# Attention in four layers on one core: keys gathered ahead of values and turned two steps ahead, the weights' loads put into the hand-kept order, a copy of the tokens moved

## The chip, the cores and the metric

The kernel runs on one core of a Trainium2 chip. Its time is the device time of one execution in microseconds (us). The engines are TensorE (PE, with its weight loads PEld), VectorE (DVE), ScalarE (ACT), GpSimd (POOL) and SyncE (SP), which issues most of the DMAs. POOL issues the gathers.

## The reference

```python
x = x + _L0_ffn_ref(_L0_cond_ref(x, ...), ...)
x = x + _L1_ffn_ref(_L1_cond_ref(x, ...), ...)
x = x + _L2_ffn_ref(_L2_cond_ref(x, ...), ...)
x = x + _L3_ffn_ref(_L3_cond_ref(x, ...), ...)
```

The tokens x are 8 sequences of 128 tokens with 512 features, float32. Each layer is a conditioning part and a feed-forward part with low-rank experts. The change is about `_L2_cond_ref`, attention with a paged cache:

```python
def _L2_cond_ref(x, Wq, Wk, Wv, Wo, q_norm_w, k_norm_w, k_cache, v_cache, block_table, cache_seqlens):
    D, HQ, HK = (128, 32, 8)
    PAGES, PSIZE, NPP = (64, 32, 16)
    ...
    q = _rope(_rmsnorm(q, q_norm_w), pos); k = _rope(_rmsnorm(k, k_norm_w), pos)
    L = NPP * PSIZE
    kc = k_cache[block_table].reshape(bsz, L, HK, D)
    vc = v_cache[block_table].reshape(bsz, L, HK, D)
    k_all = jnp.concatenate([kc, k], axis=1)
    v_all = jnp.concatenate([vc, v], axis=1)
    ...
    scores = jnp.einsum('bqhd,bkhd->bhqk', q, k_all) * SCALE
    scores = jnp.where(valid[:, None, None, :], scores, -1e+30)
    probs = jax.nn.softmax(scores, axis=-1)
    o = jnp.einsum('bhqk,bkhd->bqhd', probs, v_all)
    return jnp.einsum('bse,de->bsd', o.reshape(bsz, seqlen, HQ * D), Wo)
```

Per sequence there are 512 cached keys and values and 128 new ones, 32 query heads and 8 key heads.

## The kernel before, in words

Layers 0 and 1 come first (to about 330 us of the span), then attention, then the feed-forward part of layer 2 and layer 3. Attention is written out in 32 steps: 8 key heads (`qd`), and for each the 4 pairs of sequences (`p`, two sequences j = 0, 1). Step n works on `steps[n]`; `S[n]` holds its tiles. One key head has 4 query heads.

A step of `run` (L1227), in the order of TensorE's work:
- `weigh(n, 0)` (L1091): five score tiles `st` of the first sequence, four of cached keys `kT` and one of the new keys `kn` (in the profile `kTn`), against the queries `qT`. ScalarE takes the exponentials to `pT`, VectorE adds them up (`added`, L1113, tiles `part`).
- `project(n+1)` (L980): queries, keys and values of the next step, as a seven-product scheme for 2x2 blocks (`seven`, L932, PSUM tiles `q_one`, `q_six`, `q_five`, three buffers of the tag `mm`). Each block sum is taken from PSUM by VectorE or ScalarE in a fixed place; the dictionary `at` names calls that come between the products ("six", "u1", "u2", "c22", "c11", "c12"). The row sums of step n (`summed`, `inverted`, `spread`: a reciprocal `rr`, four copies to `R`, three DMAs that spread `R` over the partitions, one to `sums`) stand in these places too, and so does `turn_cached(n+1)` at "c22".
- `rotate(n+1)` (L1021): rotary embedding, products of POOL (`vq`, `vk`) and of VectorE (`r`), put together by `rotated` and `normed` inside the next part.
- `leave(n-1)` (L1169): the product with Wo of the step before, again with seven products (`wo_one`, `wo_two`, `wo_six`). At its "c22" stands `turn(n+1)` (L1077): VectorE transposes 32x32 blocks to `qkt`, SP writes them in four DMAs to a DRAM array `turned_new` and reads them back as `qT` and `kTn`.
- `weigh(n, 1)` with the value products `av` of the first sequence between its score tiles, the second sequence's sums, and its value products.

The cached keys come by `gather(n, "k")` (L887): 8 indirect DMAs of POOL into `kn`, two buffers. `turn_cached(n)` (L1061) transposes them on VectorE to `kt` (one buffer, shared with `qkt`), writes `turned_cached` and loads `kT` (two buffers). `gather(n, "v")` brings the values into `vals`. Before, POOL's order in a step is: `vq`, `vk` of n+1, two additions to `y`, values of n+1, keys of n+2.

Weights: `weights(qd)` (L876) loads three parts of one tile `q7` (Wk 256 KB, Wq 1 MB, Wv 256 KB) for the next head; `factors` (L867) makes four differences of blocks on VectorE. `out_weights(qd)` (L882) loads 1 MB of Wo, with four differences of its own. Both tiles have one buffer. `combine` (L904) makes four such sums of the tokens or of the outputs.

What sets the order: a scheduler of the tile layer places instructions on each engine by its own estimate of when they can start, but those wrapped in `kept(...)` are to stay in program order among themselves:

```python
def kept(i):
    return tc.keep_in_program_order(i) if running or i.ins.engine == pool.engine else i
```

`running` is filled when the step loop starts. Before, the weights' loads are not wrapped, while the DMAs of `turn`, `turn_cached` and `spread` are. `kept_x` (L716) is a copy of x in DRAM, 2 MB, for a second path that is taken only when a row sum is out of range.

Of the kernel before, what the change touches and what calls it, by code (L numbers as in the profile page):

```python
# [17 lines left out]
P = 128  # L18
# [29 lines left out]
def forward(ctx: ExitStack, tc: tile.TileContext, a: dict, out: bass.AP):  # L48
# [615 lines left out]
    with psa:  # L664
# [48 lines left out]
        mix1(1, small_bank)  # L713
        outs1(1, range(DC), large_bank)
        kept = nc.dram_tensor("kept_x", (P, DC, NT), F32, kind="Internal").ap()
        sp.dma_start(kept, x)  # L716
        c1.close()
        cl = ExitStack()
        late = cl.enter_context(tc.tile_pool(name="late", bufs=1, side="right"))
# [6 lines left out]
            lambda shape, name: ww.tile(shape, F32, tag="q7", name=name),  # L726
            lambda shape, name: ww.tile(shape, F32, tag="qs", name=name), chunks, mm,
        )
        y2 = att.run(late, end, bank)
        c2.close()  # L730
        c3 = ExitStack()
        w3 = c3.enter_context(tc.tile_pool(name="w3", bufs=1, reuse_waits="tile"))
# [51 lines left out]
def attention(tc, a, x, ident, lens, kvrow, part, ww, wop, ypool, sums, rot, eps, psa, c2, chunks, mm):  # L784
# [75 lines left out]
    def blocks(dst_pool, tag, name, n):  # L860

        raw = dst_pool.tile([P, 4, 2 * n], F32, tag=tag + "7", name=name)
        sums_ = dst_pool.tile([P, 4, 2, n], F32, tag=tag + "s", name=name + "_s")
        b11, b12, b21, b22 = (raw[:, 2 * i : 2 * i + 2, j * n : (j + 1) * n] for i in range(2) for j in range(2))
        t1, t2, t3, t4 = (sums_[:, k] for k in range(4))

        def factors():  # L867
            for o, l, r in ((t1, b12, b11), (t2, b22, t1), (t3, b22, b12), (t4, b21, t2)):
                kept(dve.tensor_tensor(o, l, r, ALU.subtract))

        return SimpleNamespace(raw=raw, factors=factors, B=(b11, b21, b22, t1, t2, t3, t4))

# [2 lines left out]

    def weights(qd):  # L876
        W[qd] = w = blocks(ww, "q", f"q7_{qd}", KW)
        sp.dma_start(w.raw[:, :, 0:HD], chunks(a["WkT"])[:, :, qd * HD : (qd + 1) * HD])
        sp.dma_start(w.raw[:, :, HD : HD + 2 * HW], chunks(a["WqT"])[:, :, qd * REP * HD : (qd + 1) * REP * HD])
        sp.dma_start(w.raw[:, :, HD + 2 * HW :], chunks(a["WvT"])[:, :, qd * HD : (qd + 1) * HD])  # L880

    def out_weights(qd):  # L882
        h0 = qd * REP * HD
        WO[qd] = w = blocks(wop, "o", f"o7_{qd}", HW)
        sp.dma_start(w.raw, a["WoT"][h0 : h0 + REP * HD, :].rearrange("(h p) o -> p h o", p=P))

    def gather(n, what):  # L887
        qd, p = steps[n]
# [15 lines left out]
    def combine(t, a11, a12, a21, a22):  # L904

        s1, s2, s3, s4 = (t[:, k] for k in range(4))
        for o, l, r, op in (
            (s1, a21, a22, ALU.add), (s2, s1, a11, ALU.subtract),
            (s3, a11, a21, ALU.subtract), (s4, a12, s2, ALU.subtract),
        ):  # L910
            kept(dve.tensor_tensor(o, l, r, op))
        return a11, a12, a22, s1, s2, s3, s4

    kept_sums = {}

    def tokens(n):


        qd, p = steps[n]
        b = 2 * p  # L920
        if 0 < qd < NQ - 1 and p in kept_sums:
            S[n]["A"] = kept_sums[p]
            return
        parts = [x[:, 2 * h : 2 * h + 2, (b + j) * P : (b + j + 1) * P] for j in range(2) for h in range(2)]
        if 0 < qd < NQ - 1:
            if not kept_sums:
                late.append(late[0].tile([P, NP, 4, 2, P], F32, tag="yT", name="xs_all"))
            S[n]["A"] = kept_sums[p] = combine(late[1][:, p], *parts)
        else:
            S[n]["A"] = combine(wk.tile([P, 4, 2, P], F32, tag="xs", name=f"xs_{n}", bufs=1), *parts)  # L930

    def seven(A, B, name, u, two, out2, out4, c11, c12, c21, c22, at):  # L932

# [87 lines left out]
    def rotate(n):  # L1021

        both = wk.tile([P, 2 * REP + 2, HD], F32, tag="r", name=f"r_{n}", bufs=1)
        views = {"q": both[:, 0 : 2 * REP], "k": both[:, 2 * REP :]}

        def terms(m, t, nh):

            full, part_ = [P, 2, nh, HD], [P, 2, nh, 64]
            ws, wx = (w[:, pair(n), :] for w in tabs[m])
            r = views[m].rearrange("p (j h) d -> p j h d", j=2)  # L1030
            u = wk.tile(full, F32, tag="v" + m, name=f"v{m}_{n}", bufs=1)
            for lo, hi in ((0, 64), (64, 0)):
                kept(pool.tensor_tensor(  # L1033
                    u[:, :, :, lo : lo + 64], t[:, :, :, hi : hi + 64],
                    wx[:, :, lo : lo + 64].unsqueeze(2).to_broadcast(part_), ALU.mult,
                ))
            kept(dve.tensor_tensor(r, t, ws.unsqueeze(2).to_broadcast(full), ALU.mult))
            return r, u

        for m, nh in (("q", REP), ("k", 1)):  # L1040
            S[n]["r" + m] = terms(m, S[n][m], nh)
        S[n]["both"] = both
# [34 lines left out]
    def turn(n):  # L1077

        s = S[n]
        m = 2 * REP  # L1080
        t = wk.tile([P, 4, m + 2, 32], F32, tag="kt", name=f"qkt_{n}", bufs=1)
        kept(dve.transpose(t, s["both"].rearrange("p m (b d) -> p b m d", b=4)))  # L1082
        s["qT"] = wk.tile([P, 4, m, 32], F32, tag="qT", name=f"qT_{n}", bufs=1)
        s["kn"] = wk.tile([P, 2, 4, 32], F32, tag="kTn", name=f"kTn_{n}", bufs=1)
        written(turned_new[n], t)
        src = turned_new[n].rearrange("b i a m d -> (b i) a m d")
        kept(sp.dma_start(s["qT"], src[:, :, 0:m, :]))
        for j in range(2):
            kept(sp.dma_start(s["kn"][:, j], src[:, :, m + j, :]))
# [71 lines left out]

    def outputs(n):
        oT = S[n]["oT"]
        S[n]["oA"] = combine(
            late[0].tile([P, 4, 2, P], F32, tag="os", name=f"os_{n}"),
            *(oT[:, j, 2 * h : 2 * h + 2, :] for j in range(2) for h in range(2)),
        )

    def leave(n, at={}):  # L1169

# [34 lines left out]
    def begin():  # L1205
        weights(0)
        out_weights(0)
        gather(0, "k")
        gather(0, "v")
        gather(1, "k")  # L1210
        W[0].factors()

    def first(n):
        tokens(n)
        project(n)
        if n == 0:
            turn_cached(n)
        for j in range(2):
            squares(n, "q", j, range(REP))
            squares(n, "k", j, range(1))  # L1220
        rotate(n)
        roots(n)
        rotated(n)
        normed(n)
        turn(n)

    def run(pool_, end, bank):  # L1227
        late.append(pool_)
        y2 = ypool.tile([P, NB, D], F32, tag="y", name="y2")
        Y.append(y2)  # L1230
# [3 lines left out]
        running.append(True)  # L1234
        end.prepare(bank)
        tokens(2)
        WO[0].factors()
        for n, (qd, p) in enumerate(steps):

            after = n + 1 if 0 < n < len(steps) - 1 else None  # L1240
            sums_of, turned_next = added(n, 0), lambda: n + 1 < len(steps) and turn_cached(n + 1)
            weigh(n, 0)
            if n:
                divided(n - 1, 1)
            for _ in sums_of:
                pass
            if n:
                outputs(n - 1)
            if after:
                project(after, {  # L1250
                    "six": lambda: summed(n, 0), "u1": lambda: inverted(n, 0), "u2": lambda: spread(n, 0),
                    "c22": turned_next, "c11": lambda: (squares(after, "k", 0, (0,)), squares(after, "q", 0, (0, 1))),
                    "c12": lambda: squares(after, "q", 0, (2, 3)),
                })
                rotate(after)
                leave(n - 1, {
                    "one": lambda: (
                        squares(after, "q", 1, range(REP)), squares(after, "k", 1, (0,)), roots(after),
                    ),
                    "c22": lambda: (rotated(after), normed(after), turn(after)),  # L1260
                })
            else:
                summed(n, 0)
                inverted(n, 0)
                spread(n, 0)
                turned_next()
                if n:
                    leave(n - 1)
            if after:
                if n + 2 == len(steps):  # L1270
                    end.load_w2()
                    end.load_aw()
                    end.shifted()
                gather(after, "v")
                if n + 2 < len(steps) and steps[n + 2][1] == 0:
                    weights(steps[n + 2][0])
            if n and p == 0:
                out_weights(qd)
            mixed = mix(n, 0)
            some = lambda: next(mixed)  # L1280
            weigh(n, 1, {2: (some,), 3: (some,), 4: (some, some, some)})
            for _ in added(n, 1):
                pass
            divided(n, 0)
            summed(n, 1)
            inverted(n, 1)
            spread(n, 1)
            for _ in mix(n, 1):
                pass
            if n + 2 < len(steps):  # L1290
                gather(n + 2, "k")
                if n:
                    if steps[n + 2][1] == 0:
                        W[steps[n + 2][0]].factors()
                    tokens(n + 2)
            if n and p == 0:
                WO[qd].factors()

            if qd == NQ - 1 and p:
                for j in range(2):  # L1300
# [2 lines left out]
                end.low(0, bank)  # L1303
                end.anchors(0, bank)
        divided(n, 1)
        outputs(n)
        end.product(0, "st", bank)
        leave(n)
        return y2
# [762 lines left out]
```

## Time and profile before

| | us |
|---|---|
| median of the runs (3) | 1788.15 |
| lowest, highest | 1774.12, 1791.17 |
| profiled execution, its own time | 1762.12 |
| its span | 1759.9 |
| step 1's first score, step 31's first score | 371.9, 1567.6 |

Mean granted clock of TensorE: 0.956.

```profile
PEclk9999999899999999999999898999999899999999
DMA  8110012335443434444443334345443433432001
L897 POOL DMA_INDIRECT kn<-in_k_cache,kvrow_k x256 | 264.0, 1031 | 81.8 <-issue 77.6
L897 POOL DMA_INDIRECT vals<-in_v_cache,kvrow_v x256 | 267.4, 1044 | 73.2 <-issue 58.8
L1066 DVE STREAM_TRANSPOSE kt<-kn 128x512 f32<-128x512 f32 x64 | 43.2, 695 | 42.0 <-DMA kn<-in_k_cache,kvrow_k 42.0
```

The rows of digits cut the span into 40 slices of 44 us: granted clock in tenths (9 is 0.9 or more), and the mean busy share of 16 DMA engines. A row of the groups reads: line, engine, operation, what is written and from what, count, busy time in us and mean ns of one, then the engine's idle time just ahead of these instructions and what ended most of it. In lists of waits the numbers are total us, how often, and the longest. In timelines they are the start and the length in us; the bracket at the end tells the idle time before and what ended it.

### The profile page before, as it was taken

The page shows a single profiled execution, that of the slowest core. Times are in us where ns is not written, and L with a number is a line of the kernel's source. Part 1 is how long each engine was busy: PE and PEld are TensorE (multiplying, and loading weights), DVE is VectorE, ACT ScalarE, POOL GpSimd, SP SyncE. Part 2 cuts the span into 40 slices and gives each one's busy share as a digit, 9 for nine tenths or more (in the row PEclk, how much of TensorE's full clock was granted, in tenths as well). Part 3 has the DMA queues.
Part 4 walks back from the last instruction along what each step waited for, and adds up shares of the span by engine and source line. Part 5 has one row for each costly group of instructions (what it writes and reads, how often), then busy time and mean ns, then how long its engine had stood idle before and what let it go on. Part 6 is the DMA issues. An engine that isn't in the chain of part 4 may idle for free.

```text
span 1759.9 us, 18914 instructions
## 1 busy us (share of the span) xinstructions
PE 1600.0 (91%) x5985; PEld 942.3 (54%) x5985; DVE 1106.2 (63%) x2123; ACT 536.5 (30%) x1324; POOL 858.6 (49%) x778
## 2 busy tenths in 40 slices
PE   9999999789889898999889798989989898989998
PEld 7887874344445444544445354544445454557753
DVE  5565333757867677777676577777767677764141
ACT  1111010433334334433334333443334333330110
POOL 2332035436666655666566555656665566540000
PEclk9999999899999999999999898999999899999999
DMA  8110012335443434444443334345443433432001
GB/s 280 37 43 10 1 47 79 107 89 138 109 121 89 129 95 119 132 106 120 108 129 92 112 91 126 100 123 139 112 119 87 127 92 110 103 111 76 1 12 38
DMA packets 161357, 169.92 MB, mean 97 GB/s; under 512 B 55712, under 2 KB 128608, under 8 KB 161120
## 3 DMA queue, kind: packets, MB, share of 16 engines
q1 hardware_dynamic: 143104, 131.61, 27.1%
q0 software_dynamic: 17056, 36.49, 7.1%
q8 instruction: 50, 0.82, 0.2%
q10 hardware_dynamic: 1088, 0.52, 0.1%
q14 instruction: 59, 0.48, 0.1%
HBM read 113.89 MB, written 42.07 MB: 89 GB/s over the span
## 4 chain that ended last, share of the span: by engine, by line
PE 57%; DVE 13%; POOL 6%; issue 6%; another core or an unknown queue 6%; DMA 6%; ACT 4%; SPq 2%; ACTq 0%; DVEq 0%; POOLq 0%
PE st L1099 11%; PE av L1150 8%; PE g L362 6%; DVE part L1119 5%; PE q_six L946 4%; PE dn L362 4%; PE q_five L946 3%; DMA qT<-turned_new 3%; PE q_one L946 2%; PE eo_l L53 2%; POOL vk L1033 2%; PE wo_one L946 2%; DVE qkt L1082 2%; PE wo_two L946 2%
## 5 line engine op out<-in xcount | busy, mean ns | idle before, releaser
L1099 PE MATMUL st<-qT,kT 128*128 128x512 f32 x512 | 274.8, 676 | 69.4 <-DMA qT<-turned_new 63.3
L1103 ACT ACTIVATE pT<-st,hide 128x512 f32<-128x512 f32 x256 | 176.0, 687 | 432.5 <-PE st L1099 286.2
L897 POOL DMA_INDIRECT kn<-in_k_cache,kvrow_k x256 | 264.0, 1031 | 81.8 <-issue 77.6
L897 POOL DMA_INDIRECT vals<-in_v_cache,kvrow_v x256 | 267.4, 1044 | 73.2 <-issue 58.8
L1150 PE MATMUL av<-pT,vals 128*128 128x512 f32 x640 | 298.9, 597 | 0.0
L1099 PEld LDWEIGHTS st<-qT,kT 128*128 128x128 f32 x512 | 110.0, 219 | 204.6 <-issue 132.3
L1033 POOL TENSOR_TENSOR vq<-q,txq 128x512 f32<-128x512 f32 x64 | 118.4, 1869 | 199.3 <-DVE q L995 177.5
L1150 PEld LDWEIGHTS av<-pT,vals 128*128 128x128 f32 x640 | 119.0, 190 | 144.1 <-issue 144.1
L1119 DVE TENSOR_TENSOR part<-pT 128x512 f32<-128x512 f32 x128 | 113.2, 886 | 128.2 <-ACT pT L1103 110.7
L1187 POOL TENSOR_TENSOR y<-y,uo 128x512 f32<-128x512 f32 x32 | 51.6, 1611 | 177.2 <-DVE y L1179 177.1
L1160 DVE TENSOR_TENSOR oT<-av,R 128x512 f32<-128x512 f32 x64 | 44.2, 691 | 93.4 <-DMA R<-R 70.2
L946 PE MATMUL wo_one<-o,oT 128*128 128x256 f32 x256 | 71.1, 402 | 27.0 <-ACT k L1000 25.0
L946 PE MATMUL q_one<-q,x 128*128 128x384 f32 x256 | 93.0, 486 | 0.0
L1000 ACT COPY q<-q_one 128x256 f32<-128x256 f32 x32 | 11.9, 372 | 250.4 <-remote 117.1
L1019 ACT ACTIVATE sqq<-q 128x128 f32<-128x128 f32 x256 | 79.3, 310 | 22.8 <-DVE q L995 16.3
L1134 DVE RECIPROCAL rr<-sum 128x128 f32<-128x128 f32 x64 | 60.9, 952 | 37.4 <-PE q_five L946 15.3
L946 PEld LDWEIGHTS wo_one<-o,oT 128*128 128x128 f32 x256 | 50.0, 200 | 46.1 <-ACT k L1000 31.8
L946 PEld LDWEIGHTS q_one<-q,x 128*128 128x128 f32 x256 | 48.5, 190 | 39.8 <-issue 14.4
L946 PE MATMUL q_six<-q_s,xs_all 128*128 128x384 f32 x192 | 69.8, 486 | 0.0
L1066 DVE STREAM_TRANSPOSE kt<-kn 128x512 f32<-128x512 f32 x64 | 43.2, 695 | 42.0 <-DMA kn<-in_k_cache,kvrow_k 42.0
L946 PE MATMUL wo_two<-o_s,os 128*128 128x256 f32 x256 | 64.9, 399 | 1.2 <-DVE vals L995 1.2
L1140 DVE COPY R<-rr 32x128 f32<-32x128 f32 x256 | 63.3, 247 | 3.7
(394 smaller groups left out, 2812.8 us busy)
## 6 DMA issues: line engine op xcount, KB each, us to landing
turned_new<-qkt SPq DMA_DIRECT2D x128, 160.0 KB
turned_cached<-kt SPq DMA_DIRECT2D x128, 128.0 KB
kT<-turned_cached SPq DMA_DIRECT2D x32, 512.0 KB
qT<-turned_new SPq DMA_DIRECT2D x32, 512.0 KB
R<-R SPq DMA_DIRECT2D x192, 64.0 KB
q<-in_WqT SPq DMA_DIRECT2D x8, 1024.0 KB
o<-in_WoT SPq DMA_DIRECT2D x8, 1024.0 KB
kn<-in_k_cache,kvrow_k POOLq DMA_INDIRECT x256
```

The lines of the kernel that those rows point to most:

```text
L362: pe.matmul(o, lhsT, rhs, start=start, stop=stop, skip_group_check=True)
L897: kept(pool.indirect_dma_start(out=d[:, c, :], out_offset=None, in_=kc if what == "k" else vc, in_offset=bass.IndirectOffsetOnAxis(ap=kvro ...
L946: kept(pe.matmul(o, l[:, c, :], r[:, c, :], start=start and c == 0, stop=c == 1, skip_group_check=True))
L1019: kept(act.activation(sq, S[n][m][:, j, i, :], AF.Square, accum_out=S[n]["ssq"][:, j, col : col + 1]))
L1033: kept(pool.tensor_tensor(u[:, :, :, lo : lo + 64], t[:, :, :, hi : hi + 64], wx[:, :, lo : lo + 64].unsqueeze(2).to_broadcast(part_), ALU ...
L1099: kept(pe.matmul(ps, s["kT"][:, c, 4 * j : 4 * j + 4, :] if c < 4 else s["kn"][:, j], s["qT"][:, :, REP * j : REP * (j + 1), :].rearrange( ...
L1103: kept(act.activation(pT[:, c, :, :].rearrange("p i t -> p (i t)"), ps, AF.Exp, **(dict(bias=hide[:, b, c : c + 1]) if c < 4 else dict(bia ...
L1119: kept(dve.tensor_tensor(o, l, r, ALU.add))
L1134: kept(dve.reciprocal(r, S[n]["sum", j]))
L1140: kept(dve.tensor_copy(R[0:32, i * P : (i + 1) * P], r[32 * i : 32 * i + 32, :]))
L1150: kept(pe.matmul(ps, v[:, c, :], pT[:, c, :, :].rearrange("p i t -> p (i t)"), start=c == 0, stop=c == NC - 1, skip_group_check=True,))
L1187: kept(pool.tensor_tensor(t, t, u.unsqueeze(1).to_broadcast([P, 2, HW]), ALU.add))
```

## The change

- `gather(n+2, "k")` moves from the end of step n to just after `rotate(n+1)`, ahead of POOL's additions to `y` and of the values' gather.
- `turn_cached(n+2)` stands at the end of step n, after the second value products; before, `turn_cached(n+1)` stood inside step n's projection.
- `turn` is split: the reads of `qT` and `kTn` are a function `fetch`, called after `leave`.
- The weights' loads are wrapped in `kept`: `weights` stands after `rotate` (before: after the values' gather), `out_weights` at the end of a head's first step (before: ahead of the value products), and its four differences are dealt out one by one over the next step.
- `combine` of the outputs is dealt out too: two of its four operations come between the additions of the exponentials.
- POOL's products `vq` are issued per sequence: four of 128x256 for two of 128x512.
- `kept_x` is copied at the end of step 3 and not ahead of the loop.
- The first steps: keys of step 1 are gathered and turned within `first`.

```diff
-        sp.dma_start(kept, x)
...
-        y2 = att.run(late, end, bank)
+        y2 = att.run(late, end, bank, lambda: sp.dma_start(kept, x))
...
     def weights(qd):
-        sp.dma_start(w.raw[:, :, 0:HD], chunks(a["WkT"])[:, :, qd * HD : (qd + 1) * HD])
...
+        for m, width in (("Wk", HD), ("Wq", REP * HD), ("Wv", HD)):
+            kept(sp.dma_start(
+                w.raw[:, :, at : at + width], chunks(a[m + "T"])[:, :, qd * width : (qd + 1) * width]
+            ))
+            at += width
     def out_weights(qd):
-        sp.dma_start(w.raw, a["WoT"][h0 : h0 + REP * HD, :].rearrange("(h p) o -> p h o", p=P))
+        kept(sp.dma_start(w.raw, a["WoT"][h0 : h0 + REP * HD, :].rearrange("(h p) o -> p h o", p=P)))
...
-            for lo, hi in ((0, 64), (64, 0)):
+            for b in ((slice(0, 1), slice(1, 2)) if nh > 1 else (slice(0, 2),)):
+                for lo, hi in ((0, 64), (64, 0)):
+                    to = u[:, b, :, lo : lo + 64]
...
         written(turned_new[n], t)
+
+    def fetch(n):
+        s = S[n]
+        m = 2 * REP
         src = turned_new[n].rearrange("b i a m d -> (b i) a m d")
         kept(sp.dma_start(s["qT"], src[:, :, 0:m, :]))
...
     def first(n):
...
-        if n == 0:
-            turn_cached(n)
+        turn_cached(n)
...
         rotate(n)
+        gather(n + 1, "k")
...
+        if n == 0:
+            fetch(n)
...
             weigh(n, 0)
+            sums_of, outs = added(n, 0), iter(())
             if n:
                 divided(n - 1, 1)
-            for _ in sums_of:
-                pass
-            if n:
-                outputs(n - 1)
+                outs = outputs(n - 1)
+            next(sums_of)
+            some(outs, 2)()
+            every(sums_of)
             if after:
                 project(after, {
-                    "six": lambda: summed(n, 0), "u1": lambda: inverted(n, 0), "u2": lambda: spread(n, 0),
-                    "c22": turned_next, "c11": lambda: (squares(after, "k", 0, (0,)), squares(after, "q", 0, (0, 1))),
+                    "six": lambda: summed(n, 0),
+                    "u1": lambda: (some(wo_ops)(), every(outs), inverted(n, 0)),
+                    "u2": lambda: (spread(n, 0), some(wo_ops)()),
+                    "c11": lambda: (squares(after, "k", 0, (0,)), squares(after, "q", 0, (0, 1))),
                     "c12": lambda: squares(after, "q", 0, (2, 3)),
                 })
+                some(wo_ops)()
                 rotate(after)
+                if n + 2 < len(steps):
+                    if steps[n + 2][1] == 0:
+                        weights(steps[n + 2][0])
+                    gather(n + 2, "k")
                 leave(n - 1, {
...
+                    "u2": lambda: every(wo_ops),
                     "c22": lambda: (rotated(after), normed(after), turn(after)),
                 })
+                fetch(after)
             else:
...
-                turned_next()
                 if n:
                     leave(n - 1)
+                else:
+                    fetch(1)
...
                 gather(after, "v")
-                if n + 2 < len(steps) and steps[n + 2][1] == 0:
-                    weights(steps[n + 2][0])
-            if n and p == 0:
-                out_weights(qd)
...
+            every(mix(n, 1))
+            if n and p == 0:
+                out_weights(qd)
+                wo_ops = WO[qd].factors()
             if n + 2 < len(steps):
-                gather(n + 2, "k")
+                turn_cached(n + 2)
                 if n:
                     if steps[n + 2][1] == 0:
-                        W[steps[n + 2][0]].factors()
+                        every(W[steps[n + 2][0]].factors())
                     tokens(n + 2)
-            if n and p == 0:
-                WO[qd].factors()
+            if n == 3:
+                kept(keep())
```

`every` runs a generator to its end, `some(ops, k)` gives a call that takes the next k of its operations.

## The prediction

> **What bounds the kernel now.** I read the page first, then the list of waits inside the attention stage (405 to 1567 us), then SP's, PE's and VectorE's timelines of two neighbouring steps.
>
> ```profile
> PE 1600.0 (91%) x5985; PEld 942.3 (54%) x5985; DVE 1106.2 (63%) x2123; ACT 536.5 (30%) x1324; POOL 858.6 (49%) x778
> PE st L1099 <- DMA qT<-turned_new: 57.0, 14, 5.4
> PE wo_one L946 <- ACT k L1000: 25.0, 11, 2.9
> DVE kt L1066 <- DMA kn<-in_k_cache,kvrow_k: 34.2, 14, 3.1
> ```
>
> TensorE sets the pace, and its stalls are few and regular. Fourteen times, at every odd step's start, the first score waits for the turned queries. In even steps the first `wo_one` waits for the projection's results to be taken from PSUM. The releaser named there, ACT, is only the last of several: VectorE, in the same stretch, stands at the cached keys' turn until a gather lands.
>
> The windows view of steps 12, 13, 14, 15 (columns: length, then each engine's busy time with its count, clock, DMA share, GB/s):
>
> ```profile
> 798.57:841.38 42.81, 35.72 (x113) 19.19 (x111) 28.93 (x52) 14.95 (x37) 27.87 (x27) 0.94 0.42 124
> 841.38:877.46 36.08, 35.93 (x112) 19.34 (x113) 25.77 (x46) 15.05 (x37) 19.75 (x18) 0.93 0.37 95
> 877.46:918.63 41.17, 34.57 (x113) 17.87 (x111) 30.43 (x51) 14.94 (x37) 27.77 (x25) 0.99 0.48 136
> 918.63:956.20 37.57, 36.92 (x112) 19.35 (x113) 26.41 (x47) 15.06 (x37) 22.30 (x21) 0.92 0.37 97
> ```
>
> Even steps take 41 to 43 us, odd ones 36 to 38, and the odd ones run at 0.92 to 0.93 of the clock. A cut to be seen: an even step's length contains the wait that ends it. Where it comes from, in step 12 (VectorE, SP, PE):
>
> ```profile
> 815.29 0.71 DVE L1066 STREAM_TRANSPOSE kt<-kn 128x512 f32<-128x512 f32 x1 [2.93 <-DMA kn<-in_k_cache,kvrow_k]
> 815.35 1.89 PE L946 MATMUL wo_one<-o,oT 128*128 128x256 f32 x4 [2.00 <-PE q_six L946]
> 825.91 2.33 SPq L1075 DMA_DIRECT2D turned_new<-qkt  x4
> 834.49 1.78 SPq L1142 DMA_DIRECT2D R<-R  x3
> 836.91 0.17 SPq L1087 DMA_DIRECT2D qT<-turned_new  x1
> 841.38 1.22 PE L1099 MATMUL st<-qT,kT 128*128 128x512 f32 x1 [4.61 <-DMA qT<-turned_new]
> ```
>
> The queries were written out by 828.24, yet SP first stood at `R<-R`, which is due only when the step's last reciprocals exist (834.49). Step 13 has `qT` ahead of `R`:
>
> ```profile
> 865.97 1.51 DVE L1082 STREAM_TRANSPOSE qkt<-r 128x1280 f32<-128x1280 f32 x1
> 871.80 0.59 SPq L1087 DMA_DIRECT2D qT<-turned_new  x1
> 877.47 1.88 PE L1099 MATMUL st<-qT,kT 128*128 128x512 f32 x4
> ```
>
> Step 14 starts with no wait. In the order of the built program, R stands before qT only in steps p=0 and p=2, just those in which a weights' transfer outside the kept order lies nearby.
>
> [...] after the wait of 4.61 us ten score matmuls take 6.82 us (841.38 to 848.20) and not 4.29, and clock means of 0.92 recur after each such wait. Waits of 2.0 to 2.9 us have it only in some steps. [...] from qT's issue to the first score are 4.47 us (836.91 to 841.38). [...] Here `vq` halves of equal size take 1.45 to 2.28 us, so that pieces may cost more or less beside VectorE.
>
> **The change, part by part.** A stall-free step: from step 13's `q_one` (848.20) to the next step's first score (877.47) 29.27, and five score tiles of 2 x 0.43 = 4.29 before it: 33.6 us. I count "pace time" from 843.91, which is 848.20 less 4.29.
>
> (a) Weights, kept order. PE's and ScalarE's instruction orders are unchanged. On SP every step now has turned_new, qT, kTn, R, except the last, where W2 and Aw still come outside the kept order and R stays first. With it a turn ending at 825.9 has qT issued 4.3 us later (867.48 to 871.80), and scores 4.5 us after that: 834.7, before PE's end of work at 836.77. Gone: 57.0 us of waits, plus the slow clock behind each: 14 x 2.4 (step 13: 2.5; step 14 shows the clock at 0.99 without it) = 34. Not gone at the last step: R's second issue ends near pace time 32.5, qT lands near 37 against 33.6, with the clock +6.
>
> (b) Keys gathered ahead of values, turned at the step's end two steps ahead. VectorE loses 1.3 us of transposes and up to 2.9 of waiting in the tight stretch. Gone: the wo_one waits, 25.0 and 2.0; slow clock after about four of them [...] 6.6; eight q_six waits of about 0.45, 3.5; in even steps another 1.0 us beyond the named waits (41.17 less 0.34, 0.14, 2.74, 3.38 is 34.6), of which I take 10 in all. Sum 47. New place: keys' gather starts after vq and vk, pace time about 18; 8 x 1.25 is 28, landed 29.7 (812.72+0.94 to 815.29: 1.6). VectorE asks for it after the copies to R, at 31.3: nothing waits, by 1.6 us. Behind that turn stand the weights' factors and then `oT`, which waits for R until 35.3 anyway. Values' gather goes to pace time 7 of the next step; first use is near 22. POOL's additions to y move from 25 to 28, and `uo` is wanted again near 38. The turned_cached stores are issued near 33.7, and kt's buffer is wanted again near 55.
>
> (c) vq in two halves per side: POOL, 4 pieces of 0.93 (half of 1.87) to 1.17 (the 128x256 addition at L1182). The first pair can start 2.5 us sooner, so only the 0.35 us wait for vk goes. Take 0; bounds -0.4 to +1 a step, hidden by the additions that stand before `r<-r,vq`.
>
> (d) WO's load at the p=0 step's end, its four factors (0.69 each) inside p=1's projection and product. The 1 MB, at the 307 GB/s of window 823:830, is about 3.5 us after an issue near 34, landed about 39.5; the first factor comes at 42.7. VectorE's chain in p=1 gets 2.1 before `uo` and 0.7 after, less the 1.3 of the keys' turn: `uo` ends 863.2 for 861.68, and PE's second wo_two wanted it at 862.10. Cost 1.7 (0 to 3) x 7 = 12. The turn then ends at pace time 25.1, scores possible at 34.0, PE's end 35.3: covered.
>
> (e) W's three loads before turned_new, after PE's last use at about 14: 1.5 MB at 309 GB/s (740:747) is 5 us[...], up to 8: done by 24.4, the turn's stores begin at 23.6. Under 1 us, cover 1.2; if lost, 1 us. With the keys' turn before them W's factors end near 36.5 and push the next step's additions by 0.6: 8 x 0.6 = 4 (0 to 8).
>
> (f) `kept_x` from 327.99 to the end of step 3: 2 MB at 354 GB/s, 6 us, beside transfers that have over 15 us to spare. At its old place turned_new's four issues took 4.46 instead of 1.9. But the keys' turn now stands before step 1's qkt and shares its buffer, so qkt waits about 4 us for the stores; step 0's additions and sum follow it. I take -2 (from -10 to +6).
>
> Sum for the profiled execution: 57 + 34 + 47 + 2 = 140, less 12 + 6 + 4 = 22, is 118; 1762.1 (span 1759.9 and 2.2 around it) becomes 1644. The runs shown have a median of 1788.15, 26 us over it with the same work, so that is waiting too. 30 steps from 371.9 to 1567.6 are 1195.7, 188 over 30 x 33.6. The 138 that (a) and (b) remove are 73% of that; of the 26 I let 17 go. 1788.15 less 118 and 17 is 1653; I say **1655**.
>
> What stays is seen too: VectorE waits 6.77 us at `rr` in step 16 for something the profile doesn't name, and 3 to 4 us in steps 26 and 30.
>
> **Rivals.**
> - *Queries are still last.* qT is ready at 32.4 against 33.6. If the loads in (e) and the inserts in (d) make it 3.2 us later, each of 30 starts waits 2 us, and half of them lose 1.7 of clock: 60 + 25, giving 1740. For it: a slack of 1.2 only. Against: step 14's start with no wait. Chance 0.15.
> - *All irregular stalls go too*, since VectorE is never late: another 48 of the 50 us that (a) and (b) leave. 1655 - 48 gives 1607. Against: the unnamed waits. 0.13.
> - *The keys land too late at the step's end.* [...] It lands 10.8 later, at 40.5; VectorE's queue (`oT`, part, sum) can hide that until about 35, so 5.5 us a step, 30 x 5.5 = 165: 1655 + 165 = 1820. It decides from an issue of about 2.5 on. [...] Against: issues beside VectorE's additions at 1.25 to 1.5. 0.06.
> - *It does not do what it says*: R still ahead of qT. The built order speaks against it except in the last step. Then only (b) stays, 47 less 22: 1763. 0.02.
>
> **How the numbers follow.** The forecast has 0.64, with its own range of 1620 to 1690. 1600 to 1740 takes in the first two rivals and leaves out the others and the tails. Faster by over 1% 0.91, within 1% 0.03, slower by over 1% 0.06; 1% is about what a measurement of this kernel can tell from no change.
>
> **What would show it.** Right: `st` waiting for qT falls from 57 to under 15 us; kt waiting for kn under 10; steps of 33.6 to 35.3 without alternation, p=1 the longest; mean clock above 0.97. Wrong: starts that still wait for qT with R behind it (slack misjudged), a kt wait near pace time 31 (gather too late), factors of WO waiting for a DMA, or step 0 to 1 growing by more than 6.

## The result: 1612 us, a tenth less than before

| | before | after |
|---|---|---|
| median of the runs (4 each) | 1785.74 | 1612.24 |
| lowest, highest | 1774.12, 1791.17 | 1608.79, 1615.59 |
| profiled execution | 1762.12 | 1615.59 |
| first score of step 1, of step 31 | 371.9, 1567.6 | 374.4, 1420.2 |

The ratio is 0.9036 with a 95% interval of 0.8983 to 0.9089; in a second set of runs 0.9029 (0.8972 to 0.9086). The kernel before differs from set to set (medians of 1785.74, 1757.71, 1786.57 and 1740.97), the kernel after does not (1612.24, 1610.73), so each experiment is read against what ran beside it. The sets of the experiments ran on three different chips; what makes the kernel before differ between them is not shown.

From the page of after, the engines (before: in the prediction) and the granted clock (before: above):

```profile
PE 1543.0 (96%) x5985; PEld 925.5 (57%) x5985; DVE 1078.4 (67%) x2123; ACT 537.9 (33%) x1324; POOL 850.3 (53%) x842
PEclk9999999979999999999999999999999999999999
```

The same TensorE instructions are busy for 57 us less (1600.0 before): the mean clock rose from 0.956 to 0.987. The windows view from the first score of step 1 to that of step 31, before and after (length, busy time and count of PE, PEld, DVE, ACT and POOL, clock, DMA share, GB/s):

```profile
371.90:1567.63 1195.73, 1077.86 (x3424) 573.03 (x3425) 854.95 (x1505) 451.54 (x1112) 738.63 (x654) 0.95 0.41 113
374.38:1420.17 1045.79, 1017.40 (x3426) 554.56 (x3424) 825.94 (x1504) 452.93 (x1112) 730.35 (x714) 1.00 0.46 131
```

Of the 150 us that these 30 steps lose, 60 are TensorE's busy time, with the faster clock, and 90 are its waits (117.9 before, 28.4 after). The list of waits of after, 405 to 1500 us (total, times, longest):

```profile
DVE oT L1179 <- DMA R<-R: 34.7, 19, 2.8
PE sum L1146 <- DVE part L1138: 14.7, 17, 2.7
PE wo_two L959 <- DVE uo L974: 8.5, 9, 2.1
DVE kt L1081 <- DMA kn<-in_k_cache,kvrow_k: 3.0, 7, 0.7
PE st L1118 <- DMA R<-R: 2.0, 1, 2.0
```

The 57.0 us in which scores waited for the queries and the 25.0 of `wo_one` are gone; the one late start (2.0 us) is step 31's, the only one with R ahead of qT. `kt` waits 3.0 instead of 34.2. The windows view of steps 12 to 15 of after (length, five engines, clock, DMA share, GB/s):

```profile
751.73:785.45 33.72, 33.53 (x114) 18.29 (x113) 25.36 (x48) 15.05 (x37) 23.92 (x25) 1.00 0.41 114
785.45:820.71 35.26, 34.02 (x114) 18.11 (x113) 27.91 (x52) 15.05 (x37) 24.97 (x25) 1.00 0.48 139
820.71:854.38 33.67, 33.48 (x114) 18.30 (x112) 25.71 (x48) 15.06 (x37) 23.88 (x25) 1.00 0.56 160
854.38:888.71 34.33, 33.42 (x114) 18.39 (x113) 28.36 (x51) 15.06 (x37) 24.54 (x25) 1.00 0.41 112
```

The alternation of 42 and 36 us is gone. What is left shows the four kinds of step: p=0 and p=2 at the pace, p=1 with WO's factors 1.5 longer, p=3 with W's factors 0.6 longer. SP and PE at the end of step 12:

```profile
774.59 1.94 SPq L1090 DMA_DIRECT2D turned_new<-qkt  x4
779.61 0.58 SPq L1106 DMA_DIRECT2D qT<-turned_new  x1
784.28 1.84 SPq L1161 DMA_DIRECT2D R<-R  x3
785.44 3.60 PE L1118 MATMUL st<-qT,kT 128*128 128x512 f32 x8
```

qT is issued 5.83 us ahead of the first score that reads it, R after it. With the 4.47 us that this trip took in step 12 of before, 1.3 us are to spare here, and 0.5 at the next start (815.69 to 820.70).

### The profile page after: what moved, and what is told of

Its sections match the earlier page's. It is cut to its first block, busy times and chain, and to the rows that moved or that the text cites. A ratio compares the mean times of both kernels' runs of the same rounds, so it can differ in the third digit from the quotient of the medians.

```text
span 1613.7 us, 18969 instructions
## 1 busy us (share of the span) xinstructions
PE 1543.0 (96%) x5985; PEld 925.5 (57%) x5985; DVE 1078.4 (67%) x2123; ACT 537.9 (33%) x1324; POOL 850.3 (53%) x842
## 4 chain that ended last, share of the span: by engine, by line
PE 70%; DVE 12%; issue 7%; POOL 4%; DMA 4%; SPq 2%; ACT 1%; DVEq 0%; ACTq 0%; POOLq 0%
PE st L1118 11%; PE av L1169 11%; PE g L362 7%; PE q_six L959 5%; PE q_five L959 5%; PE dn L362 4%; PE wo_two L959 4%; DVE part L1138 3%; PE q_one L959 3%; PE wo_six L959 3%; PE wo_one L959 2%; PE z L53 2%; PE h L1672 2%; POOL kn L904 2%; PE o L53 2%
## 5 line engine op out<-in xcount | busy, mean ns | idle before, releaser
L904 POOL DMA_INDIRECT kn<-in_k_cache,kvrow_k x256 | 294.0, 1149 | 75.8 <-issue 67.9
L904 POOL DMA_INDIRECT vals<-in_v_cache,kvrow_v x256 | 261.1, 1020 | 73.6 <-issue 68.6
L1118 PE MATMUL st<-qT,kT 128*128 128x512 f32 x512 | 241.8, 606 | 10.3 <-DMA qT<-turned_new 8.3
L1048 POOL TENSOR_TENSOR vq<-q,txq 128x256 f32<-128x256 f32 x128 | 120.4, 969 | 198.9 <-ACT sqq L1032 134.9
L1118 PEld LDWEIGHTS st<-qT,kT 128*128 128x128 f32 x512 | 99.0, 194 | 121.7 <-issue 116.1
L1138 DVE TENSOR_TENSOR part<-pT 128x512 f32<-128x512 f32 x128 | 87.4, 685 | 39.9 <-issue 23.7
L1159 DVE COPY R<-rr 32x128 f32<-32x128 f32 x256 | 84.8, 331 | 3.7
L959 PEld LDWEIGHTS q_one<-q,x 128*128 128x128 f32 x256 | 48.5, 190 | 39.8 <-issue 14.5
L1118 PE MATMUL st<-qT,kTn 128*128 128x512 f32 x128 | 65.4, 592 | 0.0
L1207 POOL TENSOR_TENSOR y<-y,uo 128x512 f32<-128x512 f32 x32 | 40.9, 1277 | 45.4 <-DVE y L1199 44.9
L362 PE MATMUL g<-xs,ws 128*128 128x256 f32 (+1 forms) x240 | 55.2, 379 | 1.5 <-POOL ws L429 1.5
```

The lines of the kernel that those rows point to most:

```text
L362: pe.matmul(o, lhsT, rhs, start=start, stop=stop, skip_group_check=True)
L904: kept(pool.indirect_dma_start(out=d[:, c, :], out_offset=None, in_=kc if what == "k" else vc, in_offset=bass.IndirectOffsetOnAxis(ap=kvro ...
L959: kept(pe.matmul(o, l[:, c, :], r[:, c, :], start=start and c == 0, stop=c == 1, skip_group_check=True))
L1048: kept(pool.tensor_tensor(to, t[:, b, :, hi : hi + 64], wx[:, b, lo : lo + 64].unsqueeze(2).to_broadcast(list(to.shape)), ALU.mult,))
L1118: kept(pe.matmul(ps, s["kT"][:, c, 4 * j : 4 * j + 4, :] if c < 4 else s["kn"][:, j], s["qT"][:, :, REP * j : REP * (j + 1), :].rearrange( ...
L1138: kept(dve.tensor_tensor(o, l, r, ALU.add))
```

## Experiments

The first question was whether the two large parts of the sum, the queries' order (a) and the keys' gather (b), are what they were priced at, and whether they add up. The first four kernels ran as one set, beside the kernel before at 1757.71.

**Order alone, at the old places.** In the kernel before:

```
-        sp.dma_start(w.raw[:, :, 0:HD], chunks(a["WkT"])...)
+        kept(sp.dma_start(w.raw[:, :, 0:HD], chunks(a["WkT"])...))
...      and so for the other three loads of W and WO
```

> The kernel before, with nothing changed but that the weights' four transfers take part in the kept order at their old places, so that every step but the last has qT ahead of R on SP. Theory T1 (the two parts add up, as the prediction's sum has it): (a) alone is worth its 57 us of waits and 34 us of slow clock, so about 1671 us profiled, 1680 to 1700 as a run; st waits for qT under 8 us, kt waits for kn about 34 us as before. Rival T2 (the parts hold each other up: the keys' gather was late in even steps only, because the wait for the queries at every odd start gave it time; with that wait gone the gather is late in every step): kt waits for kn about 3 us in every step, 80 to 100 us in all, wo_one waits about twice their 25 us, and only 40 to 60 us are won, 1725 to 1745 us.

Measured: 1768.24 us, 1.006 of before (1.004 to 1.0079): nothing is won, 10 us are lost. From step 2 on no start waits for qT, and yet a step takes 40.2 us on the mean (steps 2 to 30). VectorE's timeline in the steps 13 and 14 of this kernel, and a line of TensorE's waits:

```profile
851.78 0.69 DVE L869 TENSOR_TENSOR o_s<-o 128x512 f32<-128x512 f32 x1 [5.72 <-issue]
904.61 0.71 DVE L1066 STREAM_TRANSPOSE kt<-kn 128x512 f32<-128x512 f32 x1 [2.92 <-DMA kn<-in_k_cache,kvrow_k]
PE sum L1127 <- DVE part L1119: 46.0, 15, 5.4
```

In odd steps WO's and W's factors now stand waiting, because in program order their loads come behind turned_new, qT and kTn (WO is issued 34.9 us into step 12 here, 23.9 in before), and TensorE's first sum waits for the additions behind them (46.0 us in 15 waits). In even steps the keys' gather is as late as ever. Both theories fell short: the gather's lateness is there, as the rival said, but the larger part of what ate the gain is the loads' old place: those 46.0 us, beside 22.0 of `wo_one`. With the loads at their old places, keeping the order wins nothing.

**R ahead of qT again**, everything else as after:

```
                 leave(n - 1, {...})
-                fetch(after)
+                if p % 2: fetch(after)
...
             spread(n, 1)
+            if after and p % 2 == 0: fetch(after)
```

> The kernel after, with one thing undone: in steps p=0 and p=2 the reads of qT and kTn are issued after the copies of R instead of before them. If the place of R is the whole of part (a), the first score of 14 to 15 odd steps waits 4 to 5 us for qT and the clock halves behind each: +57 and +34 us, about 1700 us. Rival (the keys' late gather was what made those starts late, the order of SP only the last sign of it): under 20 us more than after.

Measured: 1704.69, 95 us more than the 1609.25 of the next but one kernel of the same set, which equals after. From the list of waits:

```profile
PE st L1118 <- DMA qT<-turned_new: 84.3, 14, 7.0
```

14 odd starts wait 6.0 us each; odd steps run at 0.92 to 0.96 of the clock. Undone from the finished kernel, the place of R alone costs what (a) was put at (91). The parts of the 91 are not right, though: the waits are 84.3 us and not 57, and TensorE's busy time in steps 1 to 30 is 25 us longer (1042.7 for 1017.4), where 34 were put down for the clock. About 17 us of other waits go, so that steps 1 to 30 take 93 us more. Against before, the change without (a) wins 53 us (0.9697, interval 0.9666 to 0.9729).

**Keys gathered behind the values, turn at the step's end:**

```
-                    gather(n + 2, "k")
                 leave(n - 1, {...})
...
                 gather(after, "v")
+                if n + 2 < len(steps): gather(n + 2, "k")
```

> The kernel after, with the keys' gather back behind the values' gather, the turn still at the step's end. The turn is asked for near pace time 31; the gather of values starts near 18, the keys' 8 issues of 1.25 us follow near 28 and land near 40. If the turn's wait is real, VectorE stands about 8 to 9 us at kt in every step with oT, the additions and the next projection behind it, of which the present slack before the first sum hides about 4: 4 to 5 us a step, +120 to +150 us, about 1745 us, kt waits for kn over 200 us. Rival (VectorE has enough slack there to hide all of it): within 15 us of after.

Measured: 2047.73, 438 us more than the next kernel, three times what was expected. Its waits from 405 to 1500 us (step 31 starts at 1855.2 here):

```profile
DVE kt L1081 <- DMA kn<-in_k_cache,kvrow_k: 360.8, 44, 12.6
PE sum L1146 <- DVE part L1138: 177.9, 22, 13.3
```

A step takes 48 to 51 us. The wait is not hidden, since it closes a ring: the gather stands behind the values' gather and GpSimd's additions, these wait for VectorE's `uo`, which comes, a step on, behind the turn, and the turn waits for the gather. In step 13 the second half of the turn starts at 966.62, TensorE's first sum, after a wait of 12.70, at 971.47, `uo` is complete at 985.1, the additions start at 991.48 and the values' gather at 994.41. The expectation had subtracted a slack that a ring doesn't have. A late landing of the keys, which the prediction had as a rival, is dear; what makes them late here is the order on GpSimd, and not slow issues as in that rival.

**Keys' turn back inside the projection, gather left ahead:**

```
+                    "c22": lambda: turn_cached(after),
...
-                turn_cached(n + 2)
```

> The kernel after, with the keys' turn back inside the next projection, behind q_six; the keys' gather stays ahead of the values'. Theory (what mattered in (b) is that the gather is early, not where VectorE turns): kt finds its data there, the turn costs VectorE 1.3 us before the values and u of the projection are taken, of which p=1, with the factors of WO in the same stretch, shows the most: 0 to 1 us a step, 1610 to 1645 us. Rival (the turn's place is worth as much as the gather's): wo_one waits come back at over 0.8 us a step, +40 us or more.

Measured: 1609.25 (1605.54 to 1615.88), no more than after. With the gather early, the place of the turn is worth nothing. All of (b) is that the gather is early.

**(a) without (b), at the new places of the loads:** the kernel above, and besides

```
                 rotate(after)
...
-                    gather(n + 2, "k")
                 leave(n - 1, {...})
...
                 gather(after, "v")
...
             every(mix(n, 1))
+            gather(n + 2, "k")
```

It ran in a second set, with after at 1610.73 and before at 1786.57.

> Part (a) without part (b), in the code of after: the weights' transfers and factors stay where the change puts them and qT stays ahead of R, but the cached keys are gathered behind the values at the step's end and turned inside the next projection, as in the kernel before. If (a) and (b) add up, this loses what (b) was put at, 47 us: about 1660 us. Rival, formed after the first four runs (with the wait at the odd starts gone, the keys' gather no longer gets time to catch up): from the gather's end at pace time 48 and the turn wanted at 45, the first wo_one waits about 2.8 us in every step and the clock halves behind a third of these waits, 37.5 us a step, about 1700 us; with the 1704.69 of the opposite experiment both parts are then worth more together than the sum of each alone.

Measured: 1767.91, so 157 us more than after: beyond both theories. 0.9897 of before (0.9831 to 0.9963). The expected `kt` and `wo_one` waits are there (32.0 and 14.5 us), but the largest part of the loss has another name. One line of the waits from 405 to 1500 us, and step 13:

```profile
PE q_five L959 <- DVE uq L974: 75.9, 13, 6.6
855.23 0.56 DVE L972 TENSOR_TENSOR uq<-q_six,uq 128x384 f32<-128x384 f32 x1 [6.57 <-remote]
854.78 0.94 POOL L904 DMA_INDIRECT kn<-in_k_cache,kvrow_k  x1 [0.30 <-issue]
860.17 2.93 PE L959 MATMUL q_five<-q,xs_all 128*128 128x384 f32 x4 [6.62 <-DVE uq L974]
```

VectorE stands 6.57 us before an addition whose matmuls the trace shows as ended at 849; TensorE then waits for it. Such waits of more than 3 us before `uq` or `rr`, to which the profile gives no name or that of a matmul long ended, occur 18 times in this kernel (87 us), three times in before (steps 16, 26, 30) and never in after, and 11 of the 18 end within 1 us of the start of one of the keys' gather's last issues, the others within 3.7. That they go with a gather that runs on into the projection is shown by counting; the kernel with the keys behind the values, whose gather is late too but over before VectorE takes up the projection, has none. How the gather holds them up is not shown.

**WO loaded earlier, its factors at the step's end** (with after and e5 in one set):

```
                 fetch(after)
+                if p == 0: out_weights(qd)
...
+            if n and p == 0: every(WO[qd].factors())
```

> The kernel after, with part (d) changed: WO's transfer is issued right behind the reads of qT and kTn in steps p=0, and its four factors stand at that step's end again, in the 2.7 us in which VectorE waits for R after the keys' turn. If the factors inside p=1's projection are what makes p=1 1.5 us longer (wo_two 0.62, q_six 0.44, and the rest), p=1 falls from 35.3 to about 33.8 us and the run by 10 to 12 us. Rival (the factors only push the additions and the next sum, as W's do in p=3): p=1 stays at 34.3 or more and under 7 us are won.

Measured: 1644.37, 34 us more than after. p=1 grew to 38 to 42 us:

```profile
790.68 0.62 SPq L888 DMA_DIRECT2D o<-in_WoT  x1
799.18 0.75 DVE L868 TENSOR_TENSOR o_s<-o 128x512 f32<-128x512 f32 x1 [3.90 <-DMA o<-in_WoT]
```

From issue to first use are 8.5 us beside the transfers of that stretch, not the 5.5 to which the prediction's times come, taken from the best bandwidth of a window. VectorE waits 3.90 for it with `oT` and the additions behind. The place inside p=1's projection, for all its 1.5 us, was the better one; neither theory saw that.

**A first version meant to be faster**, with that early WO and

```
-    pool.memset(b16, 0.0)
+    pool.memset(b16[:, 8:16], 0.0)
...
-        sp.dma_start(W["2"], chunks(a["W2T"]))
+        tc.keep_in_program_order(sp.dma_start(W["2"], chunks(a["W2T"])))
...      and so for Aw
         gather(0, "v")
+        gather(1, "k")
...
         rotate(n)
-        gather(n + 1, "k")
+        if n:
+            gather(n + 1, "k")
...
             every(added(n, 1))
+            some(w_ops)()
             divided(n, 0)
...
-                        every(W[steps[n + 2][0]].factors())
+                    every(w_ops)
```

> A version meant to be faster than after: WO early as in the run before; one of W's four factors ahead of the second half's division, so that three are left at the step's end (p=3 from 34.3 to 33.8, 4 us in all); W2's and Aw's transfers in the kept order, so that qT is ahead of R in the last step too (2 us and its clock); and at the start the first keys' gather of step 1 ahead of the copy of values into place as before, with b16's load freed from the memset it waited for, so that turned_new(0) is issued near 330 and not at 335.6 (up to 5 us, if the first sum does not take the wait over). 1588 to 1604 us. Rival (what is freed at the start is taken over by the next wait, step 0's additions behind the second keys' turn): 1598 to 1606 us.

Measured: 1634.64, slower than after by 24, from the same WO waits. Its other parts can be read apart: p=3 steps fell from 34.3 to 33.5, and step 0's start came at 338.93 for 344.75, but then

```profile
355.21 0.66 PE L1146 MATMUL sum<-part,ones 128*32 128x128 f32 x8 [10.12 <-DVE part L1138]
```

the first sum took the wait over, as its rival said. After itself, once more, in this set:

> The kernel after, unchanged, on the same chip as the other three, so that their few us are compared within one set of runs: 1609 to 1616 us.

Measured: 1610.73 (1610.29 to 1612.29).

**Undoing (c)**, in a third set with the next three (before: 1740.97):

```
-            for b in ((slice(0, 1), slice(1, 2)) if nh > 1 else (slice(0, 2),)):
+            for b in (slice(0, 2),):
```

> The kernel after, with part (c) undone: vq again in one instruction for each half of a head. Theory: the halves bring nothing that is not hidden, within 4 us of after. Rival: the products come 0.3 us later to the rotation in every step, and with the turn's slack of about half a microsecond some starts wait for qT, +10 us.

Measured: 1645.82, 38 us more than the kernel with the copy moved back below (1608.12), which equals after. Hardly a start waits for qT; in three steps of four it is the first sum that waits (from 405 to 1400 us 38.7 us, for 14.7 in after up to 1500). The list's line, and the end of step 12 without the split, POOL, VectorE, PE:

```profile
PE sum L1146 <- DVE part L1138: 38.7, 25, 3.2
791.56 1.27 POOL L1207 TENSOR_TENSOR y<-y,uo 128x512 f32<-128x512 f32 x1
790.97 3.13 DVE L1159 COPY R<-rr 32x128 f32<-32x128 f32 x4
802.49 0.43 PE L1146 MATMUL sum<-part,ones 128*32 128x128 f32 x8 [1.44 <-DVE part L1138]
```

and the same copies in after:

```profile
781.73 1.27 POOL L1207 TENSOR_TENSOR y<-y,uo 128x512 f32<-128x512 f32 x1
782.39 1.87 DVE L1159 COPY R<-rr 32x128 f32<-32x128 f32 x4
```

Whole instructions start when the last q is there, halves start earlier, so GpSimd's queue runs 1.2 us ahead. Its two additions to y then lie mostly on the reciprocal; without the split they lie on the four copies to R, which take 3.13 us instead of 1.87 (0.89 with GpSimd idle, 796.68 in after). R's transfer, `oT`, the additions and the sum follow, 1.3 to 1.4 us late. All steps agree: without the split the second half's copies take 3.1 us in every step p=0, 2 and 3 from step 2 to 27, and the first sum of the next step then waits 1.2 to 3.2 us; in steps p=1 they take 1.9, and the next sum waits 0.2 at most. In step 28 it is the other way round, and the cost with it: 1.87 and no wait without the split, 3.13 and a wait of 1.34 in after. In the trace without the split the first of the four copies takes 2.0 us, until the first addition ends, and 0.75 in after; it is shown as started 0.6 us ahead of that addition. Why copies beside an addition take longer is not shown.

**Undoing (f):**

```
         kept = nc.dram_tensor("kept_x", ...)
+        sp.dma_start(kept, x)
...
-            if n == 3:
-                kept(keep())
```

> The kernel after, with part (f) undone: kept_x copied at its old place before the attention stage. The prediction had 2 us for the move. Since turned_new(0) is held by b's load and not by the copy, and qkt(1) by its buffer: step 1's start within 2 us of 374.4, the run within 4 us of after. Rival (the copy's transfer at the start holds the stores of the turn as in before, where the four issues took 4.46 us): step 1's start 3 to 6 us later.

Measured: 1608.12 (1606.97 to 1608.79), so the run is within 4 us of after. Step 1's start is 2.2 us later than in after, but the load of `bcol`, ahead of the copy on SP, was already issued 3.2 us later (331.45 for 328.24), so that no gain of the move is to be seen. The four stores of the turn do take 4.31 us behind the copy, for 1.95 in after, as the rival said; the start is not held up by it.

**A faster version**: the diff of the first without the early WO (and with no gather at all behind `rotate` in `first`), and

```
         project(n)
-        turn_cached(n)
+        if n == 0:
+            turn_cached(n)
...
-        gather(1, "v")
...
-        tokens(2)
-        every(WO[0].factors())
...
                 spread(n, 0)
...
+                    turn_cached(1)
+                    gather(2, "k")
+                    gather(1, "v")
                     fetch(1)
+                    tokens(2)
+                    every(WO[0].factors())
```

> A version meant to be faster than after, with WO left where the change puts it: one of W's four factors ahead of the second half's division, W2's and Aw's transfers in the kept order, b16's load freed, and at the start the cached keys of step 1 turned inside step 0, behind its first reciprocals, with WO's first factors and the tokens' sums of step 2 behind them. Against after: p=3 steps 34.3 to 33.6 (5 us), the last start without its wait (2 us), step 0's start at about 339 as in the run before and its first sum waiting 2 to 4 us instead of 10.1, so that step 1 starts near 364 (10 us). 1592 to 1600 us. Rival (VectorE then stands at the keys' turn inside step 0, and its second half takes the wait over): step 1 not before 370, 1599 to 1606 us.

Measured: 1590.43 (1585.65 to 1592.96), 0.913 of the before of its set (0.909 to 0.917), 2 us below what was expected and 18 below the 1608.12 that stands for after in this set. Step 1 starts at 362.7 (12 us earlier), p=3 takes 33.6 (0.7 less), step 31 starts without a wait; the rival fell.

WO's factors on GpSimd, in this version:

```
-                wo_ops = WO[qd].factors()
+                every(WO[qd].factors(pool))
```

> The version of the run before with the four factors of WO computed on GpSimd, between its gather of values and its products of the rotation in p=1, instead of inside VectorE's projection. If p=1's 1.5 us are VectorE's 2.76 us of factors, p=1 falls to 33.8 and the run by 8 to 10 us. Rival (GpSimd takes 1.9 us a factor and its products of the rotation then come later than VectorE wants them, so that the turn of the queries, whose slack is below 1 us, is late): starts behind p=1 wait 1 to 3 us, and nothing is won, or 5 to 15 us lost.

Measured: 1597.06, 7 us slower than the version without.

```profile
782.79 3.74 DVE L1159 COPY R<-rr 32x128 f32<-32x128 f32 x3
782.74 1.27 POOL L868 TENSOR_TENSOR o_s<-o,o_s 128x512 f32<-128x512 f32 x1
787.24 1.56 PE L959 MATMUL q_six<-q_s,x 128*128 128x384 f32 x4 [1.30 <-DVE vals L1008]
```

Three copies take 3.74 us beside GpSimd's 1.27 us factors, one copy for each of these; `q_six` waits 1.3 for the values behind them. Neither theory had this one: the loss has the size of the rival's (5 to 15), but no start waits, and it is not in the rotation but again in the copies.

## Why the prediction was right, and where its steps were wrong

The direction and the range (1600 to 1740) held, but the forecast of 1655 was 43 us too high: 1612 lies below the 1620 to 1690 that went with it, in the part of the range that the rival *All irregular stalls go too* (1607) had added. For the profiled execution the sum said 118, measured are 146.5. Steps 1 to 30 took 1195.7 and take 1045.8, 37.8 over 30 times the pace of 33.6; the prediction's terms leave 66. This difference of 28 is nearly the whole error of the sum. About 20 of it is the clock: TensorE's busy time fell by 60, and the terms for the clock were 34 and 6.6. The other 8 are waits. Another 12 us are the offset between runs and profile: of its 26 the prediction let 17 go (the 73% that it names would be 19); all went, and after's median is 3 below its profile.

- **(a) 91**: 95 from the side of after, in part by luck, since the waits were longer and the clock's share smaller than put down; nothing from the side of before (order alone: +10). **(b) 47**: from the side of after 157, and only its gather. Each alone wins little: with (a) undone 53 us remain of the gain, where everything together wins 148 in that set; with (b) undone 19, where everything together wins 176. The step that failed is the plus sign between them. The sum came out near because it counted the stalls that the profile showed, and these do all go when both are made.
- The *unnamed waits* of steps 16, 26 and 30, which the prediction left standing among "50 us that (a) and (b) leave", went with the late gather; they belonged to (b)'s term.
- **(c) 0**: wrong, about 37 from the side of after. Cover was looked for ahead of `r<-r,vq`, where the pieces are used; what counted was where the rest of GpSimd's queue comes to lie against VectorE's copies. The bounds (-0.4 to +1 a step) had the size, with the wrong sign.
- **(d) 12**: right in size; the seven p=1 steps are 1.0 to 3.5 longer than 33.7, 13 in all. That the factors make these is not isolated: the runs that took them out of the projection brought new waits. Its transfer was mis-sized (5.5 us from the issue to the landing, where factors that waited for it came 6.3 to 9.1 us after the issue), and the first factor, placed at 42.7, waited 0.9 us at most.
- **(e) 4**: right: five p=3 steps are 0.6 longer, and more in steps 3 and 27, where a stretch of half clock joins it (3.413 us each, from 451.0 and from 1277.1); the faster version takes the 0.6 away. The 8 us up to which it put W's loads was an estimate, and no experiment shows it.
- **(f) -2**: wrong by about 4. From the load of `bcol` to step 1's start are 44.3 us in before, 46.1 in after and 45.1 with the copy back at its old place, so the move wins nothing that can be seen; `qkt` waits 4.37 for the shared buffer as foreseen, and step 1's start is 2.5 later. What was overlooked: b's load stands ahead of turned_new(0) on SP and waits for a memset behind the keys' gather on GpSimd (turned_new(0) at 335.60, its data ready at 329.9).
- **Last step +6**: 2.0 us of wait.
- *Queries are still last* was rightly unlikely, by less than a microsecond: the slack of 1.2 is 0.5 to 1.3. Its 1.7 us of clock behind a wait, like (b)'s 6.6 behind four, was an estimate; a single stretch of half clock in the trace of before is 3.413 us, so 1.7 are lost in it. *Keys land too late* did not come about: an issue took 1.9 us at worst (mean 1149 ns for 1031), where the rival decides from about 2.5 on. That issues beside VectorE's rotation would become that slow was an estimate, and no run shows it. That a late landing costs a great deal is shown with another cause, and far above its 165 us.

## What to carry to other kernels

Stalls that hide behind each other in one step are not to be added as if each were alone: undo each part from the finished side as well as adding it to the old one, since here the parts won 19 and 53 apart and 148 to 176 together. A transfer moved in a kept order takes its consumers' place with it, so order, load and first use must be moved as one. And what a shift on one engine is worth is read from what then lies beside it on another: four copies on VectorE took 3.13 us beside GpSimd's additions, and 0.89 with GpSimd idle.

## What the runs showed of the hardware

- Four copies of 32x128 on VectorE take 0.89 us with GpSimd idle, 3.13 beside GpSimd's additions; three take 3.74 beside GpSimd's factors.
- Where TensorE's clock is shown as lowered in steps 1 to 30, it is half, for 3.413 us or a multiple of it (3.413, 6.827 and 10.24 us in before, 3.413 twice in after). Behind a wait of TensorE of 2.1 us it is sometimes half and sometimes not: without the split, the p=3 steps 7 and 23 and step 16 with first-sum waits of 2.1 to 2.2 ran at 0.954 on the mean, steps 11, 15 and 19 with the same wait at 1.00. In steps 1 to 30 of all 14 traces, a stretch of half clock began in the wait or within 3.5 us of its end after 19 of 74 waits of 1.5 to 2.5 us, 31 of 48 of 2.5 to 3.4, 16 of 17 of 3.4 to 4, and all 83 that were longer (in before and after alone: 4 of 8, 7 of 14, 5 of 5 and 8 of 8).
- Instructions that wait for a 1 MB load of weights, among the other transfers of a step, start 6.3 to 9.1 us after its issue.
- With the keys' gather running on into the projection, VectorE and ScalarE sometimes start 5 to 6 us after the matmuls they wait for are shown as ended (in the step above `uq` at 855.23, its `q_six` ended at 849.13; ScalarE's `q` at 858.92, its `q_one` ended at 853.55). Why stays open.
